# Second layer of a graph transformer: slot sums by TensorE in place of VectorE, and the norm's inverse root by Newton steps in place of logarithm and exponential

## The chip, the cores and the metric

One core of a Trainium2 chip runs the whole program. The metric is the device time of one execution in microseconds. Engines are named as the profile names them: PE (TensorE), DVE (VectorE), ACT (ScalarE), POOL (GpSimd) and SP (SyncE, which here only issues transfers).

## The reference

A graph of 6250 nodes and 100000 edges (sorted by destination), 16 node types, 32 edge types, width 128 in 8 heads of 16. Two layers of this, then a final linear layer, a residual and a norm:

```python
def gt_layer(x, ntype, etype, src, dst, Wk, Wq, Wv, Wa, Watt, Wmsg, pri, skip, g, b):
    k = typed_linear(x, ntype, Wk).reshape(n, H, HS)
    q = typed_linear(x, ntype, Wq).reshape(n, H, HS)
    v = typed_linear(x, ntype, Wv).reshape(n, H, HS)
    kT = jnp.einsum('nhd,htdo->nhto', k, Watt)
    vT = jnp.einsum('nhd,htdo->nhto', v, Wmsg)
    kw = kT[src, :, etype]
    m = vT[src, :, etype]
    a = jnp.einsum('ehd,ehd->eh', kw, q[dst]) * pri[:, etype].T / SQRT_D
    att = edge_softmax(a, dst, n)
    msg = (m * att[:, :, None]).reshape(-1, H * HS)
    hag = jax.ops.segment_sum(msg, dst, num_segments=n)
    h = jax.nn.silu(typed_linear(hag, ntype, Wa))
    alpha = jax.nn.sigmoid(skip[ntype])[:, None]
    h = h * alpha + x * (1.0 - alpha)
    mu = jnp.mean(h, axis=-1, keepdims=True)
    var = jnp.mean((h - mu) ** 2, axis=-1, keepdims=True)
    return (h - mu) * jax.lax.rsqrt(var + 1e-05) * g + b
...
h = x
for l in range(L):
    h = gt_layer(h, ...)
return layernorm(x + (h @ ff_w + ff_b))
```

## The kernel before

**Tables and blocks.** For each layer the kernel writes a table in HBM with a row of 256 floats (transformed key and value) for each pair of node and edge type. Nodes are ranked by type class and by number of edges and put into 50 blocks of 128. A block has a fixed number of slots, K, one per edge of its node with the most edges: 25, 22, 20, 19, 18, 17, 16, 16, 15 and 14 for the ten blocks of each of four type classes, then one of 41 and nine of 13 down to 8. All blocks together have 867 slots. Blocks are taken in 15 superblocks of three or four. In order of execution their slots are [25, 22, 20, 19], [18, 17, 16], [16, 15, 14], [41, 13, 12], then a class and [12, 12, 11], a class and [11, 10, 9, 8], and the last class.

**The edge loop** (`edges`, once for each layer) goes over the blocks. A slot is one indirect gather of 128 rows of the table, issued by POOL (L987). Four slots make a chunk, a tile `kv` of which 12 exist. DVE multiplies the key halves by the query (L999) and reduces them to scores (L1003). When a block's scores are there, `finished` does the softmax over slots: mask (L898), maximum (L903), difference (L905), exponential on ACT (L908), its sum `den` (L911); then, chunk by chunk, the value halves are multiplied by the weights (L922), the chunks are added (L929), and the four remaining slots are reduced to `sums` (L932). `finished` of one block is a generator that is advanced three times for each chunk of the next block.

In the second layer a block has a tile `pair` of two PSUM banks (pool `tps`, three of them, tile name `tb`). Its second bank holds the query and, behind it, the weights; its first bank holds `acc`, the four partial sums. The first chunk is multiplied into `acc`, later ones in place in `kv`. In the first layer these stand in SBUF.

**Node steps.** When a superblock's sums are ready, `nodes` divides them by `den` (`normalized`, L1030 to L1037) and does the type-dependent product (`typed_linear`, L238 and L247, with masked copies `xm`), the activation (L1085, L1092), the skip (L1099), mean and variance (`stats`, L1066, L1069), the inverse root (`rstd_of`) and the norm (L1106, L1110). In the first layer it goes on to the second layer's keys, values and queries and, in `pieces_of`, to that layer's table: PE products (L268) into `tb`, ACT copies (L275) into `st`, scatters by POOL (L1198). In the second layer it does the final product (L1175 to L1177; L1177 adds the input row by a product with the identity), a second norm and an output scatter by POOL (L1231). These steps are advanced between the steps of the edge loop: `spread` gives a generator's steps a rate, a number of steps over the slots of a coming superblock.

**Order.** POOL's instructions stand in the order in which the program issues them. The other engines' orders are made by the scheduler when the program is built; each engine then runs its list in order and waits on semaphores.

Of the kernel before, what the change touches and what calls it, by code (L numbers as in the profile page):

```python
# [9 lines left out]
F32 = mybir.dt.float32  # L10
BF16 = mybir.dt.bfloat16
I32 = mybir.dt.int32
AF = mybir.ActivationFunctionType
ALU = mybir.AluOpType
AX = mybir.AxisListType
# [3 lines left out]
P = 128  # L19
# [4 lines left out]
LN_EPS = 1e-5  # L24

SB = 4
# [5 lines left out]
CH = 4  # L32
# [64 lines left out]
def kernel(  # L97
# [21 lines left out]
    nc = tc.nc  # L119
    N, D = out.shape  # L120
# [4 lines left out]
    L, TY, _, _ = Wk.shape  # L125
    _, H, RT, HS, _ = Watt.shape
    HP = H // 2
    TG = RT // 16
    TC = TY // NC
# [29 lines left out]
    ident = keep.tile([P, P], F32, name="ident")  # L159
# [5 lines left out]
    start = keep.tile([P, NB], I32, name="start")  # L165
# [60 lines left out]
    def superblocks(n):  # L226
        k = -(-n // SB)
        for c in range(k):
            yield n * c // k, n * (c + 1) // k - n * c // k
# [150 lines left out]
    with tc.If(unsorted > 0):  # L380
# [7 lines left out]
        with tc.For_i(0, EC, 1) as j:  # L388
            pair = pp.tile([P, 2], I32, name="pair")
# [57 lines left out]
    with tc.tile_pool(name="tp", bufs=2) as tp, \  # L447
# [304 lines left out]
        sbs = list(superblocks(NT))  # L752
# [26 lines left out]
    def arm(fast):  # L779
# [4 lines left out]
        STB = 3 if fast else 2  # L784
        ep = ctx2.enter_context(tc.tile_pool(name="ep", bufs=2))
        npl = ctx2.enter_context(tc.tile_pool(name="npl", bufs=1))
        eps = npl.tile([P, 1], F32, name="eps")
        nc.vector.memset(eps, LN_EPS)

        nps = ctx2.enter_context(tc.tile_pool(name="nps", bufs=2 if fast else 5, space=PSUM))  # L790
        tps = ctx2.enter_context(tc.tile_pool(name="tps", bufs=3, space=PSUM))
# [2 lines left out]
        sbs = []  # L794
# [7 lines left out]
        else:  # L802
            sbs = [(i0, k, range(TY)) for i0, k in superblocks(NB)]
# [40 lines left out]
        def edges(l):  # L844
# [8 lines left out]
            def spread(work, gen, steps, slots):  # L853

                work.append([gen, steps / slots, 0.0])
# [24 lines left out]
            def slots(s):  # L880
                return sum(KB[b] for b in range(sbs[s][0], sbs[s][0] + sbs[s][1]))

            def query(s, i):


                if l == 0:
                    return got[s][0][:, i, :], None
                pair = tps.tile([P, 2, SB * P], F32, name="tb")
                nc.scalar.copy(pair[:, 1, :D], got[s][0][:, i, :])  # L889
                return pair[:, 1, :D], pair  # L890

            def finished(s, i, chunks, kvt, a, pair, sums, den):


                i0, k, _ = sbs[s]
                K = KB[i0 + i]
                av = a[:, :K, :]
                nc.vector.tensor_tensor(  # L898
                    av, av, neg[:, KO[i0 + i]:KO[i0 + i] + K].unsqueeze(2)
                    .to_broadcast([P, K, H]), op=ALU.add)  # L900
                yield
                m = ep.tile([P, H], F32, name="m")
                nc.vector.tensor_reduce(m, av.rearrange("p k h -> p h k"), axis=AX.X, op=ALU.max)  # L903
                yield
                nc.vector.tensor_tensor(av, av, m.unsqueeze(1).to_broadcast([P, K, H]),  # L905
                                        op=ALU.subtract)
                w = av if l == 0 else pair[:, 1, D:D + K * H].rearrange("p (k h) -> p k h", h=H)
                nc.scalar.activation(w, av, AF.Exp)  # L908
                yield
                yield  # L910
                nc.vector.tensor_reduce(den[:, i, :], w.rearrange("p k h -> p h k"),  # L911
                                        axis=AX.X, op=ALU.add)

                if l == 0:
                    acc = ep.tile([P, CH, D], F32, name="acc", bufs=1)
                else:
                    acc = pair[:, 0].rearrange("p (k c) -> p k c", k=CH)
                for j in range(len(chunks) + 1):
                    if j < len(chunks):
                        j0, j1 = chunks[j]  # L920
                        v = kvt[j][:, :j1 - j0, D:]
                        nc.vector.tensor_tensor(  # L922
                            (v if j else acc).rearrange("p k (h d) -> p k h d", h=H),
                            v.rearrange("p k (h d) -> p k h d", h=H),
                            w[:, j0:j1, :].unsqueeze(3).to_broadcast([P, j1 - j0, H, HS]),
                            op=ALU.mult)
                    if j > 1:
                        j0, j1 = chunks[j - 1]
                        nc.vector.tensor_tensor(acc[:, :j1 - j0], kvt[j - 1][:, :j1 - j0, D:],  # L929
                                                acc[:, :j1 - j0], op=ALU.add)  # L930
                    yield
                nc.vector.tensor_reduce(sums[:, i, :], acc.rearrange("p k c -> p c k"),  # L932
                                        axis=AX.X, op=ALU.add)
                if i == k - 1:
                    spread(work, nodes(l, *sbs[s], sums, den, got[s][1], lambda gen: table(s, gen)),
                           36 if l else 27 + (12 if len(sbs[s][2]) > TC else 0), pace(s + 1))

            def pace(s):
                s = min(s, len(sbs) - 1)
                return slots(s) - 0.5 * KB[sbs[s][0]]  # L940
# [3 lines left out]
            def table(s, gen):  # L944


                if gen is None:
                    if s - 2 in tables:
                        rush(pieces, tables[s - 2])
                else:  # L950
                    tables[s] = gen
                    spread(pieces, gen, 8 * sbs[s][1] + 4, (1.0 if s + 4 < len(sbs) else 0.6) * slots(min(s + 2, len(sbs) - 1)))

            before = iter(())
            q, pair = query(0, 0)
            for s, (i0, k, types) in enumerate(sbs):
# [4 lines left out]
                sums = ep.tile([P, SB, D], F32, name="sums")  # L961
                den = ep.tile([P, SB, H], F32, name="den")
                for i in range(k):
                    b = i0 + i
                    K = KB[b]
                    a = ep.tile([P, max(KB), H], F32, name="a")
                    chunks = [(j, min(j + CH, K)) for j in range(0, K, CH)]
                    kvt = []
# [12 lines left out]
                    for j0, j1 in chunks:  # L981
                        c = j1 - j0
                        kv = ep.tile([P, CH, 2 * D], F32, name="kv", bufs=12)
                        kvt.append(kv)
                        for j in range(j0, j1):
                            at = KO[b] + j
# [3 lines left out]
                            if l == 1:  # L990
                                for put in puts:
# [13 lines left out]
                                                axis=AX.X, op=ALU.add)  # L1005
# [7 lines left out]
                    if not then:  # L1013
                        step(end=True)
                    before = finished(s, i, chunks, kvt, a, pair, sums, den)
                    q, pair = then[0] if then else (None, None)
            for _ in before:
# [25 lines left out]

        def rstd_of(mv, k):

            rs = npl.tile([P, SB], F32, name="rs")
            nc.scalar.activation(rs[:, :k], mv[:, :k, 1], AF.Ln, bias=eps)
            v = npl.tile([P, SB], F32, name="v")
            nc.vector.tensor_scalar(v[:, :k], mv[:, :k, 1], LN_EPS, -0.5, op0=ALU.add, op1=ALU.mult)
            yield  # L1050
            nc.scalar.activation(rs[:, :k], rs[:, :k], AF.Exp, scale=-0.5)
            yield
            t = npl.tile([P, SB], F32, name="t")
            nc.vector.tensor_tensor(t[:, :k], rs[:, :k], rs[:, :k], op=ALU.mult)
            yield
            nc.vector.tensor_tensor(t[:, :k], t[:, :k], v[:, :k], op=ALU.mult)
            yield
            nc.vector.scalar_tensor_tensor(rs[:, :k], t[:, :k], 1.5, rs[:, :k],
                                           op0=ALU.add, op1=ALU.mult)
            yield  # L1060
            return rs

        def stats(mv, what, k):
# [8 lines left out]
        def nodes(l, i0, k, types, sums, den, ntb, table):  # L1072
# [29 lines left out]
            yield  # L1102
            yield from stats(mv, lambda i: hs[:, i, :], k)
            rs = yield from rstd_of(mv, k)
            for i in range(k):
                nc.vector.scalar_tensor_tensor(hs[:, i, :], hs[:, i, :], mv[:, i, 0:1], gt[:, l],  # L1106
# [66 lines left out]
            for i in range(k):  # L1173
# [4 lines left out]
            yield  # L1178
            yield from stats(mv, lambda i: f[:, i * P:(i + 1) * P], k)
            rs = yield from rstd_of(mv, k)  # L1180
            o = npl.tile([P, SB * P], F32, name="o", tag="kvT0", bufs=2).rearrange(
                "p (i d) -> p i d", i=SB)
# [140 lines left out]
    with tc.If(full < 1) as cmp:  # L1323
        with ExitStack() as ctx2:
            ctx2.enter_context(tc.manual_schedule(engines={mybir.EngineType.Pool}))
            arm(True)
    with cmp.Else():
        with ExitStack() as ctx2:
            arm(False)
# [46 lines left out]
```

## Time and profile before

| | |
|---|---|
| median of 3 runs | 3465.71 us (3457.21 to 3470.19) |
| the profiled execution | 3457.21 us |
| its span | 3455.4 us |
| PE busy | 1937.8 us (56%) |
| DVE busy | 2165.0 us (63%) |
| ACT busy | 978.7 us (28%) |
| POOL busy | 2002.5 us (58%) |
| mean granted TensorE clock | 0.72 of full speed |

Busy time of an engine counts its instructions, not the gaps in which it issues or waits. Three stages follow each other: table building for the first layer to about 700 us (POOL's first table gather starts at 817 us), the first layer's edge loop to 2240 us, and the second layer's to the end. In a list of instruction groups a row gives line, engine, operation, output and input tiles, count, then busy time and mean duration in ns, then the engine's idle time ahead of them and what ended it. In the timeline a row gives start, duration, engine, line, instruction, and in brackets the idle time before it.

### The profile page before, as it was taken

The numbers are of one execution on the slowest core, as the hardware profiler recorded it, in microseconds if no ns is written. First come the engines' busy times: TensorE is split into PE (matmuls) and PEld (weight loads), VectorE is DVE, ScalarE is ACT, GpSimd is POOL, SyncE is SP. The second block draws the span as 40 slices with busy tenths as digits, with TensorE's granted clock in tenths as the row PEclk, the third lists the DMA queues.
The fourth block names the chain that finished last, engine by engine and source line by source line (L and its number), as shares of the span: only waits on it lengthen the run. The fifth ranks groups of instructions, "written<-read, shape, count | busy, mean of one in ns | idle before, by whom it ended". The sixth has DMA issues, their size and how long they took to land. (4 is left out here: it accounts for less than half of the span.)

```text
span 3455.4 us, 25373 instructions
## 1 busy us (share of the span) xinstructions
PE 1937.8 (56%) x7142; PEld 874.0 (25%) x7142; DVE 2165.0 (63%) x4496; ACT 978.7 (28%) x1594; POOL 2002.5 (58%) x2032
## 2 busy tenths in 40 slices
PE   6999999894057676777778777602112222121313
PEld 3444454332022232333233223201001111011111
DVE  5787786332575677666666765346656666566765
ACT  2444433452014313442344245401111111021111
POOL 0000003644767777767767776177767777777773
PEclk9999999995577677877777877755555555555555
DMA  7676655889338656885688478734333333333331
GB/s 198 277 301 285 273 244 213 316 343 292 99 115 290 221 189 223 292 289 189 226 290 317 164 280 328 317 107 113 110 99 109 111 112 106 111 117 110 110 106 49
DMA packets 201147, 694.53 MB, mean 201 GB/s; under 512 B 61383, under 2 KB 111897, under 8 KB 175947
## 3 DMA queue, kind: packets, MB, share of 16 engines
q0 software_dynamic: 105424, 448.83, 39.1%
q1 hardware_dynamic: 79182, 236.82, 17.8%
q10 hardware_dynamic: 16384, 7.11, 0.9%
q8 instruction: 60, 0.98, 0.1%
q14 instruction: 97, 0.79, 0.1%
HBM read 268.12 MB, written 429.48 MB: 202 GB/s over the span
## 5 line engine op out<-in xcount | busy, mean ns | idle before, releaser
L987 POOL DMA_INDIRECT kv<-tab,ell x1734 | 1708.7, 985 | 618.8 <-issue 471.4
L275 ACT COPY st<-tb 128x512 f32<-128x512 f32 (+1 forms) x976 | 681.0, 764 | 602.9 <-PE tb L268 515.9
L253 PE MATMUL nb<-ident,hag 128*128 128x128 f32 x100 | 26.1, 399 | 767.1 <-DVE hag L1037 750.9
L739 PE MATMUL l<-xm,wkqv 128*128 128x512 f32 (+1 forms) x832 | 383.1, 595 | 31.7 <-DVE xm L238 31.7
L999 DVE TENSOR_TENSOR kv<-kv,tb 128x512 f32<-128x512 f32 (+3 forms) x234 | 150.5, 645 | 381.3 <-DMA kv<-tab,ell 368.4
L999 DVE TENSOR_TENSOR kv<-kv,q 128x512 f32<-128x512 f32 (+3 forms) x234 | 151.6, 650 | 352.9 <-DMA kv<-tab,ell 345.1
L268 PE MATMUL tb<-bdv,kvT 32*128 32x512 f32 x800 | 268.4, 795 | 67.0 <-ACT st L275 65.9
L1003 DVE TENSOR_REDUCE a<-kv 128x32 f32<-128x512 f32 (+3 forms) x468 | 297.3, 638 | 2.2
L247 PE MATMUL nb<-xm,wa 128*128 128x384 f32 (+1 forms) x384 | 214.3, 720 | 83.7 <-DVE xm L238 83.6
L268 PE MATMUL tb<-bdk,kvT 32*128 32x512 f32 x800 | 241.9, 781 | 23.5 <-ACT st L275 23.1
L273 DVE COPY st<-tb 128x512 f32<-128x512 f32 (+1 forms) x208 | 149.0, 717 | 117.1 <-PE tb L268 96.0
L238 DVE SCALAR_TENSOR_TENSOR xm<-ntb,hT 128x512 f32<-128x512 int32 (+1 forms) x208 | 133.3, 656 | 131.7 <-PE l L739 103.2
L238 DVE SCALAR_TENSOR_TENSOR xm<-ntb,nb 128x384 f32<-128x384 bf16 (+1 forms) x336 | 185.6, 591 | 47.5 <-PE nb L253 31.6
L253 PEld LDWEIGHTS nb<-ident,hag 128*128 128x128 f32 x100 | 15.6, 197 | 785.3 <-issue 576.6
L739 PEld LDWEIGHTS l<-xm,wkqv 128*128 128x128 f32 x832 | 148.0, 192 | 261.8 <-issue 195.9
L1198 POOL DMA_INDIRECT tab<-st,row x100 | 107.9, 1079 | 149.4 <-ACT st L275 102.9
L727 POOL DMA_DIRECT2D ntb<-in_node_type_dram x13 | 7.3, 559 | 317.2 <-DVE xm L238 317.2
L247 PE MATMUL nb<-xm,wq 128*128 128x384 f32 (+1 forms) x192 | 104.0, 707 | 138.4 <-DVE xm L238 138.4
L268 PE MATMUL tb<-bdv,yT 32*128 32x512 f32 x784 | 169.2, 663 | 2.5 <-DVE st L273 2.2
L889 ACT COPY tb<-q 128x128 f32<-128x128 f32 x50 | 13.4, 269 | 469.8 <-DVE sums L932 346.8
L247 PEld LDWEIGHTS nb<-xm,wa 128*128 128x128 f32 x384 | 95.6, 262 | 200.1 <-DVE xm L238 115.2
L1132 PE MATMUL nb<-xm,wkqv 128*128 128x384 f32 (+1 forms) x288 | 125.2, 585 | 33.2 <-DVE xm L238 22.6
(243 smaller groups left out, 3009.6 us busy)
## 6 DMA issues: line engine op xcount, KB each, us to landing
tab<-st SPq DMA_DIRECT2D x98, 2048.0 KB, 6.7
kv<-tab,ell POOLq DMA_INDIRECT x1734
hr<-xrd SPq DMA_DIRECT2D x30, 192.0 KB, 3.9
hr<-xrd SPq DMA_DIRECT2D x15, 256.0 KB, 7.3
xrd<-xr POOLq DMA_DIRECT2D x11, 256.0 KB
hr<-in_x_dram POOLq DMA_DIRECT2D x10, 256.0 KB
ntb<-in_node_type_dram POOLq DMA_DIRECT2D x10, 256.0 KB
ntb<-typed SPq DMA_DIRECT2D x20, 96.0 KB, 3.2
```

Source lines behind the costliest of these rows:

```text
L238: nc.vector.scalar_tensor_tensor(xm[:, :n], ntb[:, :n], float(t), hT[:, :n], op0=ALU.is_equal, op1=ALU.mult)
L247: nc.tensor.matmul(ps[:, :n], w[:, t, :], xm[:, :n], start=(t == types[0]), stop=(t == types[-1]))
L253: nc.tensor.transpose(tr[:, i * P:(i + 1) * P], src_of(i), ident)
L268: nc.tensor.matmul(pt[:, b], yT[s, i * P:(i + 1) * P], bd[s, tt, :], start=True, stop=True)
L273: nc.vector.tensor_copy(to, pt)
L275: nc.scalar.copy(to, pt)
L739: nc.tensor.matmul(ps[i][:, :n], wkqv[:, i, t, :], xm[:, :n], start=(t == 0), stop=(t == TY - 1))
L987: get = nc.gpsimd.indirect_dma_start(out=kv[:, j - j0, :], out_offset=None, in_=tabs[l][:], in_offset=bass.IndirectOffsetOnAxis(ap=ell[:, ...
L999: nc.vector.tensor_tensor(kk, kk, q.unsqueeze(1).to_broadcast([P, c, D]), op=ALU.mult)
L1003: nc.vector.tensor_reduce(a[:, j0:j1, :], kk.rearrange("p k (h d) -> p k h d", h=H), axis=AX.X, op=ALU.add)
L1132: nc.tensor.matmul(outs[j][:, :n], wkqv[:, j, t, :], xm[:, :n], start=(t == types[0]), stop=(t == types[-1]))
L1198: put = nc.gpsimd.indirect_dma_start(out=tabs[1].rearrange("(n t) c -> n (t c)", t=16), out_offset=bass.IndirectOffsetOnAxis(ap=row2[:, tg ...
```

## The change

In the second layer each value chunk is multiplied in place, the first one too. The sum over slots is then one product per slot of the identity and the slot's 128 values, accumulated in the first bank of `pair`, issued in the step after the chunk's multiplication; ACT copies the result to `sums`. The adds and the reduction on DVE remain for the first layer alone. In `rstd_of`, in both layers, the logarithm and the exponential on ACT with one Newton step on DVE are replaced by an integer first guess and three Newton steps on DVE. The numbers of steps given to `spread` become 34 (27 before) and 50 (36 before).

```diff
-        eps = npl.tile([P, 1], F32, name="eps")
-        nc.vector.memset(eps, LN_EPS)
...
                 if l == 0:
                     acc = ep.tile([P, CH, D], F32, name="acc", bufs=1)
-                else:
-                    acc = pair[:, 0].rearrange("p (k c) -> p k c", k=CH)
                 for j in range(len(chunks) + 1):
                     if j < len(chunks):
                         j0, j1 = chunks[j]
                         v = kvt[j][:, :j1 - j0, D:]
                         nc.vector.tensor_tensor(
-                            (v if j else acc).rearrange("p k (h d) -> p k h d", h=H),
+                            (acc if l == 0 and not j else v).rearrange("p k (h d) -> p k h d", h=H),
                             v.rearrange("p k (h d) -> p k h d", h=H),
                             w[:, j0:j1, :].unsqueeze(3).to_broadcast([P, j1 - j0, H, HS]),
                             op=ALU.mult)
-                    if j > 1:
+                    if l == 1 and j > 0:
+                        j0, j1 = chunks[j - 1]
+                        for at in range(j0, j1):
+                            nc.tensor.matmul(pair[:, 0, :D], ident, kvt[j - 1][:, at - j0, D:],
+                                             start=(at == 0), stop=(at == K - 1))
+                    if l == 0 and j > 1:
                         j0, j1 = chunks[j - 1]
                         nc.vector.tensor_tensor(acc[:, :j1 - j0], kvt[j - 1][:, :j1 - j0, D:],
                                                 acc[:, :j1 - j0], op=ALU.add)
                     yield
-                nc.vector.tensor_reduce(sums[:, i, :], acc.rearrange("p k c -> p c k"),
-                                        axis=AX.X, op=ALU.add)
+                if l == 0:
+                    nc.vector.tensor_reduce(sums[:, i, :], acc.rearrange("p k c -> p c k"),
+                                            axis=AX.X, op=ALU.add)
+                else:
+                    nc.scalar.copy(sums[:, i, :], pair[:, 0, :D])
                 if i == k - 1:
                     spread(work, nodes(l, *sbs[s], sums, den, got[s][1], lambda gen: table(s, gen)),
-                           36 if l else 27 + (12 if len(sbs[s][2]) > TC else 0), pace(s + 1))
+                           50 if l else 34 + (12 if len(sbs[s][2]) > TC else 0), pace(s + 1))
...
         def rstd_of(mv, k):
-            rs = npl.tile([P, SB], F32, name="rs")
-            nc.scalar.activation(rs[:, :k], mv[:, :k, 1], AF.Ln, bias=eps)
             v = npl.tile([P, SB], F32, name="v")
-            nc.vector.tensor_scalar(v[:, :k], mv[:, :k, 1], LN_EPS, -0.5, op0=ALU.add, op1=ALU.mult)
-            yield
-            nc.scalar.activation(rs[:, :k], rs[:, :k], AF.Exp, scale=-0.5)
-            yield
+            nc.vector.tensor_scalar(v[:, :k], mv[:, :k, 1], LN_EPS, None, op0=ALU.add)
+            yield
+            gi = npl.tile([P, SB], I32, name="gi")
+            nc.vector.tensor_single_scalar(gi[:, :k], v[:, :k].bitcast(I32), 1,
+                                           op=ALU.arith_shift_right)
+            yield
+            ri = npl.tile([P, SB], I32, name="ri")
+            nc.vector.tensor_scalar(ri[:, :k], gi[:, :k], -1.0, float(0x5F3759DF),
+                                    op0=ALU.mult, op1=ALU.add)
+            nc.vector.tensor_scalar(v[:, :k], v[:, :k], -0.5, None, op0=ALU.mult)
+            yield
+            rs = ri.bitcast(F32)
             t = npl.tile([P, SB], F32, name="t")
-            nc.vector.tensor_tensor(t[:, :k], rs[:, :k], rs[:, :k], op=ALU.mult)
-            yield
-            nc.vector.tensor_tensor(t[:, :k], t[:, :k], v[:, :k], op=ALU.mult)
-            yield
-            nc.vector.scalar_tensor_tensor(rs[:, :k], t[:, :k], 1.5, rs[:, :k],
-                                           op0=ALU.add, op1=ALU.mult)
-            yield
+            for _ in range(3):
+                nc.vector.tensor_tensor(t[:, :k], rs[:, :k], rs[:, :k], op=ALU.mult)
+                yield
+                nc.vector.tensor_tensor(t[:, :k], t[:, :k], v[:, :k], op=ALU.mult)
+                yield
+                nc.vector.scalar_tensor_tensor(rs[:, :k], t[:, :k], 1.5, rs[:, :k],
+                                               op0=ALU.add, op1=ALU.mult)
+                yield
             return rs
```

## The prediction

> **What bounds the kernel now.** I read the busy time by stage first, because a share over the whole span mixes three stages: table building (to about 700 us), first layer (to 2240 us) and second layer (to the end).
>
> ```profile
> core 0: us, PE busy (x) PEld busy (x) DVE busy (x) ACT busy (x) POOL busy (x), PEclk, DMA share, GB/s
> 700.00:2240.00 1540.00, 1049.46 (x3222) 430.98 (x3222) 936.47 (x1914) 558.27 (x781) 1028.70 (x1002) 0.75 0.70 248
> 2240.00:3455.00 1215.00, 251.15 (x642) 147.37 (x642) 751.68 (x1812) 148.55 (x293) 873.52 (x917) 0.54 0.36 105
> ```
>
> In the second layer no engine looks full: POOL 72%, DVE 62%, PE 21%. The groups of instructions for that stretch explain POOL:
>
> ```profile
> L987 POOL DMA_INDIRECT kv<-tab,ell x867 | 822.7, 949 | 291.3 <-issue 243.2 <-DVE tb L922 8.9 <-DVE tb L929 5.0
> ```
>
> There are 867 gathers of 0.949 us, and before nearly each of them a gap of 0.30 us in which POOL waits for nothing ("issue"). So a gather costs 1.25 us: 867 x 1.25 = 1084 us, and 50 output scatters at 1.3 us add 65. That is 1149 of 1215 us; about 45 us are the tail behind the last gather, and real waits of POOL come to about 20. **POOL's issue is the bound of the second layer**; DVE, PE and ACT matter only where they release a gather buffer late, and in the tail. The timeline shows where they do (start, duration, instruction, idle time before it):
>
> ```profile
> 2541.83 0.69 DVE L922 TENSOR_TENSOR tb<-kv,tb 128x512 f32<-128x512 f32 x1
> 2542.48 0.80 PE L1175 MATMUL nb<-ffw,h 128*128 128x128 f32 x2 [0.57 <-ACT h L1171]
> 2542.55 1.28 DVE L922 TENSOR_TENSOR kv<-kv,tb 128x512 f32<-128x512 f32 x2
> 2542.79 0.94 POOL L987 DMA_INDIRECT kv<-tab,ell  x1 [7.65 <-DVE tb L922]
> ...
> 2631.99 0.67 DVE L922 TENSOR_TENSOR tb<-kv,tb 128x512 f32<-128x512 f32 x1
> 2632.93 0.94 POOL L987 DMA_INDIRECT kv<-tab,ell  x1 [1.60 <-DVE v L1049]
> 2633.23 1.27 DVE L922 TENSOR_TENSOR kv<-kv,tb 128x512 f32<-128x512 f32 x2
> 2637.47 0.94 POOL L987 DMA_INDIRECT kv<-tab,ell  x1 [2.35 <-DVE t L1056]
> ```
>
> With 12 chunk buffers, a chunk's first gather needs the chunk 12 places before it to be read for the last time. The 41-slot block (11 chunks) and the 25-slot blocks (7 chunks) run out: six waits of 7.65, 2.27, 1.60, 2.35, 1.72 and 2.35 us, of which 0.30 each is issue. I paired every chunk with its predecessor: beside these six and the chunks right behind them the margin is 2.5 us at the last 25-slot block, 8.3 at the first, and 10 us or more elsewhere.
>
> In the first layer POOL is also ahead of the others (1029 of 1540 busy, plus 0.30 us for each issue), but it has real waits, most of them in scatters of the second table:
>
> ```profile
> POOL tab L1198 <- ACT st L275: 102.9, 25, 14.7
> L1047 ACT ACT_TABLE_LOAD x6 | 7.7, 1283 | 0.1
> ```
>
> (POOL's waits from 700 to 2300 us: total, number, longest; then table loads in one window of the layer, 1300 to 1800 us: 6 of 1283 ns, as many again at L1051.)
>
> **The change, part by part.** The sum is made on the profiled execution, 3457.2 us (span 3455.4); the median of the runs is 3465.7, so 8.5 us are added at the end.
>
> *Taken from DVE in layer 2.* 185 adds (L929, 0.632 us) are 117 us and 50 reductions (L932, 0.678) are 34. Newton adds 9 instructions per norm of about 0.157 us (rows of L1054, L1056, L1058), 30 norms: 42 us. DVE falls by 109 us of 752. On the path this is worth 0: POOL's 1.25 us per gather hides it. Were POOL's gathers free, DVE would be next and the 109 us would count.
>
> *Given to PE.* 867 products of the identity with a 128x128 fp32 slot. The same shape and operands stand at L1177, among the final products:
>
> ```profile
> 3434.61 0.79 PE L1175 MATMUL nb<-ffw,h 128*128 128x128 f32 x2 [0.57 <-ACT h L1171]
> 3435.33 0.79 PE L1176 MATMUL nb<-ffb,one_row 1*128 1x128 f32 x2
> 3436.06 0.80 PE L1177 MATMUL nb<-hr,ident 128*128 128x128 f32 x2
> 3436.64 0.64 PE L1175 MATMUL nb<-ffw,h 128*128 128x128 f32 x2
> ```
>
> Nine such products take 5.99 us from 3434.61 to 3440.60 (the last one's end): 0.665 us each, 2.66 for a chunk of four. So PE gains 577 us and stands at 828 of 1215, below POOL. The other end of the price: at the first layer's higher granted clock (0.75 against 0.54) 5.5 products of 512 columns took 4.88 us (0.89 each), where second-layer ones take 1.68; half, hence 0.33 and 1.33 for a chunk. I take 0.665, the row of this shape in this stage.
>
> [...]
>
> *The new wait.* The program's waits tie both engines together through the tile that holds weights and sums: the products of chunk j wait for DVE's multiplication of chunk j+1, and the multiplication of chunk j+2 waits for those products. What queues behind a waiting multiplication is all of DVE: the next block's scores and the norms. With 0.1 us for each hand-over a link costs 2.86 us; there are 235 chunks less two per block, 135 links. If nothing lay between, DVE would wait 386 us, and 752 - 109 + 386 = 1029 is still under 1215. So DVE does not become the bound; only lateness of releases counts.
>
> *Releases.* 41-slot block: the first buffer was free at the end of its multiplication (2542.5). Now it needs the second multiplication (2543.2), then PE, whose queue has nine final products in front, from 2542.48 on (9 x 0.665, to 2548.5), then 2.66: 2551.1. The wait grows by 8.6; the later 2.27 goes (the chain then needs 3.4 us a chunk where gathers need 5.0); six more Newton steps in front cost 1. Together +8; without the queue +2, at 0.33 us about 0. 25-slot blocks: 2633.9 + 0.1 + 2.66 = 2636.6, and with the 0.30 us of issue the gather starts 5.2 us late instead of 1.3, but the second wait (2.05) goes: +1.9 each for two of them, about +1 for the one with 2.5 us of margin, 0 for the first. Sum +13. Bounds: 0, if PE runs at 0.33; +53, if at all four 25-slot blocks PE's node products (5.2 us for the type products, 6.0 for the final ones) stand in front, 4 x 11.2 + 8.
>
> *Tail.* The last block has 14 slots, chunks of 4, 4, 4, 2. Before, from its first multiplication to its sum: 3414.09 to 3419.24, 5.15 us. After: 1.25 + 2.76 + 0.65 + 2.76 + 0.4 + 2.76 + 1.43, and 0.4 for ACT's copy: 12.4, so +7.3; of the previous block's adds and reduction, 2.6 us that stood in front, I credit half: +6. At 0.33: 0. The norm itself: 13 dependent steps at 0.19 us (L1054 to L1058 start 0.19 to 0.20 apart) are 2.5 us, the chain over ACT took 2.5 (3441.54 to 3444.01): 0.
>
> *Layer 1.* ACT loses 30 table loads (38.5 us) and 30 short activations of 0.30 and 0.20 us (7.5): 46 of 558 busy us, hidden by POOL except where a scatter waits for ACT's copies. In the drain before layer 2 the norm ended at 2188.93, 6.7 us after its mean and variance (copies and two loads in ACT's queue); 2.5 now: -4.2. Of the earlier waits only that of 4.46 us at 1434 has a load and a logarithm inside it: -1.6. The node steps become 34 and 50 in place of 27 and 36 for the same slots, so some scatters move past one chunk in POOL's queue, 5 us either way. I take -6; bounds -46 (all of ACT's saving on the path) and +10 (two scatters caught early).
>
> [...]
>
> **Sum:** -6 + 13 + 6 + 0 = +13: 3470 for an execution like the profiled one, **3479** beside the median. 0.5% (17 us) is about what a measurement of this kernel can tell from no change.
>
> **Rivals.** *Slower:* PE's node products stand in front of the slot sums at every tight buffer; it decides where lateness passes the margins (0, 2.5, 8.3 us). For it: PE's order is fixed when the program is built. Against: a 25-slot block ends before the final products are due. -6 + 53 + 6 = +53: 3519. *Faster:* ACT's copies were what held the scatters, and all 46 us that ACT saves come off the 102.9 us of waits. For: 25 waits name ACT. Against: most follow type products on PE, with no load near. -46 + 13 + 6 = -27: 3439. *PE at the higher clock:* -6 + 0 + 0: 3460.
>
> **Numbers.** Chances: my sum 0.45, slower rival 0.33, faster rival 0.15, higher clock 0.07. Of my sum 0.06 lies beyond +17 and of the higher clock 0.01 beyond -17, so slower 0.39, same 0.45, faster 0.16. Range 3440 to 3525, from the faster rival to just past the slower one; about half of each of the two lies outside.
>
> **What would show it.** Second layer: gathers still 0.95 us with 0.30 before; POOL's waits now name PE's slot sums, 25 to 40 us in total in place of 20; PE about 830 busy; L929 and L932 gone; one or two table loads left. First layer: waits for ACT's copies near 100 us. It is wrong if a gather's cadence changes, if POOL waits for PE at ordinary blocks, or if the layer boundary moves by more than 15 us.

## The result

The changed kernel takes 3479.52 us (median of 20 runs, 3470.95 to 3489.29), the kernel before 3466.7 us beside it (20 runs, 3457.21 to 3476.15). The ratio is 1.0036, 95% interval [1.0026, 1.0047]: 12.8 us more, inside the 0.5% that was forecast as no change. The profiled execution took 3484.13 us (span 3482.3).

The time was met; the sum behind it was not. These are the stages of the profiled executions, read off POOL's timeline (the one before was the fastest of its 20, and 4.6 us of the difference of 26.9 between the two are the start's):

| us | before | after | foreseen |
|---|---|---|---|
| start to POOL's first table gather | 817.2 | 821.8 | 0 |
| first layer: to the second layer's first gather | 1423.0 | 1444.5 (+21.5) | -6 |
| second layer: first to last gather | 1161.6 | 1163.2 (+1.6) | +13 |
| tail: last gather to the end of the last output scatter | 46.5 | 45.5 (-1.0) | +6 |

The engines' busy times by stage, and the groups and waits of the second layer of the changed kernel, stand against the rows of before in the prediction:

```profile
core 0: us, PE busy (x) PEld busy (x) DVE busy (x) ACT busy (x) POOL busy (x), PEclk, DMA share, GB/s
700.00:2266.00 1566.00, 1050.46 (x3218) 440.47 (x3214) 949.87 (x2047) 512.07 (x718) 1045.68 (x1004) 0.74 0.69 244
2266.00:3475.00 1209.00, 609.87 (x2376) 486.05 (x2376) 648.85 (x1848) 69.52 (x223) 873.50 (x917) 0.60 0.37 105
```

```profile
L991 POOL DMA_INDIRECT kv<-tab,ell x867 | 822.7, 949 | 288.2 <-issue 217.3 <-PE tb L926 37.7 <-DVE kv L1003 4.6
...
L926 PE MATMUL tb<-kv,ident 128*128 128x128 f32 x1734 | 394.5, 404 | 470.1 <-DVE kv L918 376.4 <-issue 89.0 <-ACT hb L1100 2.5
```

```profile
POOL tab L1209 <- ACT st L275: 114.3, 25, 25.7
POOL out_dram L1242 <- DVE o L1195: 42.6, 4, 24.1
POOL kv L991 <- PE tb L926: 37.7, 81, 13.0
```

(The last three are POOL's waits: total, number, longest; the first from 700 to 2300 us, the other two in the second layer.) The edit did what it says: PE has 1734 more records (two for each of 867 products), ACT fell to 70 us, DVE from 752 to 649. The gathers are the same 867 of 949 ns. Of the 81 waits for PE's sums most are the 0.30 us of issue that were there before; the real one is that of 13.0 us. The second layer is still bound by POOL's issue, and so all this work moved at a cost of 0.6 us. What was lost was lost in the first layer, which this edit touches through the Newton steps, one step number (34 for 27) and the order that the scheduler makes of them.

### Where the second layer's numbers came from

The one long wait is the 41-slot block's (timeline of the changed kernel: start, duration, instruction, idle time before it):

```profile
2566.78 0.80 PE L1186 MATMUL nb<-ffw,h 128*128 128x128 f32 x2 [0.57 <-ACT h L1182]
...
2568.39 1.27 DVE L918 TENSOR_TENSOR kv<-kv,tb 128x512 f32<-128x512 f32 x2
...
2572.57 1.91 PE L926 MATMUL tb<-kv,ident 128*128 128x128 f32 x8
2574.52 0.69 DVE L918 TENSOR_TENSOR kv<-kv,tb 128x512 f32<-128x512 f32 x1 [0.80 <-PE tb L926]
2574.76 0.94 POOL L991 DMA_INDIRECT kv<-tab,ell  x1 [12.95 <-PE tb L926]
```

As foreseen, the nine final products stand in front of the slot sums and POOL waits for both: 12.95 + 0.63 us in place of 7.65 + 2.27, +3.7. What the second layer got in addition are two output scatters that wait, 0.80 and 4.40 us; this is the longer one:

```profile
2924.82 1.01 POOL L1242 DMA_INDIRECT out_dram<-o,node  x1 [4.40 <-DVE o L1195]
```

At the 25-slot blocks the four waits of before are gone. The first of them, DVE and ACT alone, before and after:

```profile
2621.94 0.34 ACT L908 ACTIVATE tb<-a 128x200 f32<-128x200 f32 x1
...
2623.60 0.69 DVE L999 TENSOR_TENSOR kv<-kv,tb 128x512 f32<-128x512 f32 x1 [1.25 <-DMA kv<-tab,ell]
2628.19 0.69 DVE L999 TENSOR_TENSOR kv<-kv,tb 128x512 f32<-128x512 f32 x1 [3.90 <-DMA kv<-tab,ell]
2628.79 0.55 DVE L1092 SCALAR_TENSOR_TENSOR th<-th,nb 128x384 f32<-128x384 f32 x1
2629.26 0.36 DVE L911 TENSOR_REDUCE den<-tb 128x8 f32<-128x200 f32 x1
```

```profile
2652.69 0.34 ACT L906 ACTIVATE tb<-a 128x200 f32<-128x200 f32 x1
2653.18 0.54 DVE L1103 SCALAR_TENSOR_TENSOR th<-th,nb 128x384 f32<-128x384 f32 x1
2653.64 0.36 DVE L909 TENSOR_REDUCE den<-tb 128x8 f32<-128x200 f32 x1
2653.91 0.68 DVE L918 TENSOR_TENSOR kv<-kv,tb 128x512 f32<-128x512 f32 x1
...
2658.52 0.69 DVE L1003 TENSOR_TENSOR kv<-kv,tb 128x512 f32<-128x512 f32 x1 [1.04 <-DMA kv<-tab,ell]
```

Before, the block's first weighting (2631.99) came 10.1 us after its exponential, because DVE's list put it behind two score multiplications that wait 1.25 and 3.90 us for gathers, and behind some node steps. After, it comes 1.2 us behind. That is a new order in DVE's list, made when the program is built; it pays for the longer chain through PE.

The last block, DVE's multiplication of its last chunk by the query, before and after, then the rest of the changed kernel's chain:

```profile
3409.96 0.41 DVE L999 TENSOR_TENSOR kv<-kv,tb 128x256 f32<-128x256 f32 x1
```

```profile
3432.34 0.42 DVE L1003 TENSOR_TENSOR kv<-kv,tb 128x256 f32<-128x256 f32 x1 [3.36 <-DMA kv<-tab,ell]
3435.28 0.68 DVE L918 TENSOR_TENSOR kv<-kv,tb 128x512 f32<-128x512 f32 x1
...
3437.40 6.82 PE L926 MATMUL tb<-kv,ident 128*128 128x128 f32 x38 [2.20 <-DVE kv L918]
...
3446.42 0.27 ACT L937 COPY sums<-tb 128x128 f32<-128x128 f32 x1 [2.75 <-PE tb L926]
```

From the first weighting to the sums 11.4 us, in place of 5.15 (foreseen 12.4). But the first weighting comes 5.8 us after the start of the last gather (3429.44), in place of 12.3 (3401.76 to 3414.09). Before, DVE came to the last score multiplication 8.2 us after that gather's start and had not waited; after, it sat idle for the gather and was there 2.9 us after its start. The adds and the reduction of the block ahead are 2.6 us of what no longer stands in front; its weightings and a superblock's norm and output, which stood there too, now come earlier or later in DVE's list.

### The profile page after: what moved, and what is told of

Read it like the earlier page. It is cut to its first block, busy times and chain, and to the rows that moved or that the text cites. A ratio compares the mean times of both kernels' runs of the same rounds, so it can differ in the third digit from the quotient of the medians.

```text
span 3482.3 us, 29131 instructions
## 1 busy us (share of the span) xinstructions
PE 2298.3 (66%) x8876; PEld 1222.0 (35%) x8876; DVE 2076.2 (60%) x4666; ACT 854.9 (25%) x1464; POOL 2016.5 (58%) x2032
## 5 line engine op out<-in xcount | busy, mean ns | idle before, releaser
L991 POOL DMA_INDIRECT kv<-tab,ell x1734 | 1726.4, 996 | 619.7 <-issue 447.5
L926 PE MATMUL tb<-kv,ident 128*128 128x128 f32 x1734 | 394.5, 404 | 470.1 <-DVE kv L918 376.4
L926 PEld LDWEIGHTS tb<-kv,ident 128*128 128x128 f32 x1734 | 350.8, 301 | 516.7 <-DVE kv L918 347.7
L1003 DVE TENSOR_TENSOR kv<-kv,tb 128x512 f32<-128x512 f32 (+3 forms) x234 | 151.1, 646 | 487.3 <-DMA kv<-tab,ell 473.5
L268 PE MATMUL tb<-bdv,kvT 32*128 32x512 f32 x800 | 272.9, 820 | 67.4 <-ACT st L275 66.5
L268 PE MATMUL tb<-bdk,kvT 32*128 32x512 f32 x800 | 243.4, 781 | 12.5 <-ACT st L275 12.1
L247 PE MATMUL nb<-xm,wa 128*128 128x384 f32 (+1 forms) x384 | 201.9, 687 | 61.5 <-DVE xm L238 61.5
L1209 POOL DMA_INDIRECT tab<-st,row x100 | 104.6, 1046 | 154.6 <-ACT st L275 114.3
L247 PE MATMUL nb<-xm,wq 128*128 128x384 f32 (+1 forms) x192 | 105.6, 714 | 131.9 <-DVE xm L238 122.2
L918 DVE TENSOR_TENSOR kv<-kv,tb 128x512 f32<-128x512 f32 (+3 forms) x234 | 147.4, 638 | 37.2 <-PE tb L926 37.2
L268 PE MATMUL tb<-bdv,yT 32*128 32x512 f32 x784 | 166.7, 654 | 2.9 <-ACT st L275 1.8
L247 PEld LDWEIGHTS nb<-xm,wa 128*128 128x128 f32 x384 | 92.6, 252 | 167.2 <-DVE xm L238 88.0
L1162 PE MATMUL nb<-xm,wkqv 128*128 128x384 f32 (+1 forms) x288 | 134.0, 626 | 16.6 <-DVE xm L238 16.4
```

The lines of the kernel that those rows point to most:

```text
L247: nc.tensor.matmul(ps[:, :n], w[:, t, :], xm[:, :n], start=(t == types[0]), stop=(t == types[-1]))
L268: nc.tensor.matmul(pt[:, b], yT[s, i * P:(i + 1) * P], bd[s, tt, :], start=True, stop=True)
L918: nc.vector.tensor_tensor((acc if l == 0 and not j else v).rearrange("p k (h d) -> p k h d", h=H), v.rearrange("p k (h d) -> p k h d", h=H ...
L926: nc.tensor.matmul(pair[:, 0, :D], ident, kvt[j - 1][:, at - j0, D:], start=(at == 0), stop=(at == K - 1))
L991: get = nc.gpsimd.indirect_dma_start(out=kv[:, j - j0, :], out_offset=None, in_=tabs[l][:], in_offset=bass.IndirectOffsetOnAxis(ap=ell[:, ...
L1003: nc.vector.tensor_tensor(kk, kk, q.unsqueeze(1).to_broadcast([P, c, D]), op=ALU.mult)
```

## The experiments

On record stood theory 1, the prediction's own terms, and theory 2, read from the profile after: the slot sums cost the second layer nothing, the loss is the first layer's, by the pace of its steps (2a) or by the Newton instructions and the new order they bring (2b). Times are ratios to the kernel before on the same chip; stages are from one profiled execution each. The first four ran on a chip on which the kernel before took 3898 us, so the questions were put again on two others, at 3467 and 3468 us.

**The kernel before, as it is** (before_same).

> The kernel before itself, unchanged: its ratio shows what this comparison tells from no change (1.000 within 0.001 by every theory), and its profile gives the stage times on the same chip as the kernels run beside it. The first four runs were on a chip on which the kernel before took 3898 us; there its stages were not profiled.

Ratio 0.9997 [0.9982, 1.0012]. First layer 1422.7, second 1207.9 (before: 1423.0, 1208.1): the two layers repeat within 0.3 us. How the second divides does not: its gathers took 1162.3 and its tail 45.6 (before: 1161.6 and 46.5), so the -1.0 of the table's tail is no difference, and half of its +1.6 may be none. Nor does the start repeat: 826.9 in place of 817.2, and from 817 to 829 over the profiled executions of all kernels. So ten us of difference between two spans can be the start's, and stages are compared from the first gather on.

**Slot sums on PE alone** (pe_sums, pe_sums2). The changed kernel's `edges` with the old `rstd_of` and the old step numbers:

```diff
+                    if l == 1 and j > 0:
+                        j0, j1 = chunks[j - 1]
+                        for at in range(j0, j1):
+                            nc.tensor.matmul(pair[:, 0, :D], ident, kvt[j - 1][:, at - j0, D:],
+                                             start=(at == 0), stop=(at == K - 1))
-                    if j > 1:
+                    if l == 0 and j > 1:
...
+                    nc.scalar.copy(sums[:, i, :], pair[:, 0, :D])
```

> The kernel before with the slot sums of the second layer on TensorE alone; the norm and the step numbers 36 and 27 as before. Theory 1 (the terms of the prediction: releases +13, tail +6, first layer -6): second layer longer by 19 us from its first gather to the end, first layer unchanged, ratio to before 1.0055. Theory 2 (the profile of the changed kernel: the slot sums cost the second layer nothing, what is lost is lost in the first layer): second layer within 3 us of before's 1208, first layer unchanged, ratio 0.998 to 1.001.

> The kernel before with the slot sums on TensorE alone, as in the run pe_sums, for a chip on which the kernel before takes near 3466 us. Theory 1: second layer longer by 19 us, ratio 1.0055. Theory 2: second layer within 3 us, ratio 0.998 to 1.001. On a chip like that of the first runs (3898 us, where GpSimd waited 280 us and more in the second layer): second layer longer by 25 to 35 us, ratio near 1.010 as there.

pe_sums2: 1.0009 [0.9996, 1.0022]; first layer 1426.9 (+4, though its code is that of before), second 1209.8 (gathers 1163.3, tail 46.5). Theory 1's +19 in the second layer falls. The 41-slot wait is 12.99 + 0.70 here too, and of the four 25-slot waits one of 3.67 is left: DVE's order changed with the slot sums alone. pe_sums, on the other chip: 1.0103 [1.0078, 1.0127]; second layer 1456, where the two kernels with DVE's sums run beside it took 1425. There POOL waited 314 us beyond issue in the second layer (pe_sums2: 70), and 282 and 283 in those two kernels, newton and before_pace26: on that chip the chain through PE cost some 31 us and was not free. Why that chip is slower stays open.

**Newton steps alone** (newton, newton2). The changed kernel's `rstd_of` and step numbers 34 and 50, sums on DVE.

> The kernel before with the Newton steps and the step numbers 50 and 34; slot sums on VectorE as before. Theory 1: first layer -6 us, second layer +0, ratio 0.998. Theory 2: the first layer, from its first gather to the second layer's first gather, is longer by 13 to 21 us, waits of GpSimd for the table copies of ScalarE near 114 us with one near 25 us; ratio 1.004 to 1.006.

> The kernel before with Newton steps and the step numbers 34 and 50, as in the run newton, for a chip near 3466 us. Theory 1: first layer -6 us, ratio 0.998. Theory 2: first layer longer by 10 to 21 us, second layer within 3 us, ratio 1.003 to 1.006.

newton2: 1.0002 [0.9986, 1.0019], which neither theory had. First layer 1436.6, +14 as theory 2 said, with a wait of 25.8 us like the changed kernel's; but second layer 1198.9, -9.0, as all four 25-slot waits went. newton, on the other chip: 1.0073 [1.0046, 1.0099].

The two parts explain the second layer. Both remove the same four waits of the 25-slot blocks (6.7 us beyond issue): the Newton kernel all of them, the slot sums alone half (3.4 are left), both together all of them once. Together they also have what neither has alone, the two output scatters that wait 0.80 and 4.40 us. So 3.7 - 6.8 + 4.6 = +1.5 (issue taken off), and 1.6 was measured for the gathers.

**The pace in the first layer** (before_pace26, before_pace26b): the kernel before with one number changed, so that its node steps finish at 0.85 of a superblock's slots, as in the changed kernel (29 steps at 34; before: 22 at 27, 0.81).

```diff
-                           36 if l else 27 + (12 if len(sbs[s][2]) > TC else 0), pace(s + 1))
+                           36 if l else 26 + (12 if len(sbs[s][2]) > TC else 0), pace(s + 1))
```

> The kernel before with 26 in place of 27 steps in the first layer, so that the node steps finish at 0.85 of a superblock's slots, as in the changed kernel, and nothing else. Theory 2a: first layer longer by 10 to 20 us, ratio 1.003 to 1.006. Theories 1 and 2b: ratio 1.000 within 0.002.

> The kernel before with 26 in place of 27 steps in the first layer and nothing else, as in the run before_pace26, for a chip near 3466 us. Theory 2a (pacing alone makes the loss): first layer longer by 10 to 20 us, ratio 1.003 to 1.006, near that of newton2. Theory 2b (the Newton instructions make it): ratio 1.000 within 0.002.

before_pace26b: 1.0039 [1.0026, 1.0053], first layer 1446.4 (+23.5), second 1206.7; on the other chip 1.0046 [1.0025, 1.0067]. Without a Newton step or a slot sum on PE, one number costs what the whole change costs, a little more than 2a said. The third superblock shows how, in the timeline of the kernel before (before_same), then of before_pace26b:

```profile
1023.75 2.84 ACT L275 COPY st<-tb 128x1024 f32<-128x1024 f32 x3
1024.81 2.15 PE L268 MATMUL tb<-bdv,kvT 32*128 32x512 f32 x4 [7.01 <-ACT st L275]
1026.89 13.07 PE L247 MATMUL nb<-xm,wq 128*128 128x384 f32 x32
1027.00 1.01 ACT L275 COPY st<-tb 128x1024 f32<-128x1024 f32 x1 [0.41 <-PE tb L268]
1028.29 1.99 POOL L1198 DMA_INDIRECT tab<-st,row  x1 [8.07 <-ACT st L275]
...
1045.49 1.01 POOL L1198 DMA_INDIRECT tab<-st,row  x1 [10.18 <-ACT st L275]
```

```profile
1023.84 1.93 ACT L275 COPY st<-tb 128x1024 f32<-128x1024 f32 x2 [1.42 <-PE tb L268]
1024.58 2.07 PE L268 MATMUL tb<-bdv,kvT 32*128 32x512 f32 x2
1026.58 12.51 PE L247 MATMUL nb<-xm,wq 128*128 128x384 f32 x32
1039.02 1.13 PE L268 MATMUL tb<-bdv,kvT 32*128 32x512 f32 x6
...
1042.39 1.02 POOL L1198 DMA_INDIRECT tab<-st,row  x1 [25.36 <-ACT st L275]
```

The first scatter of a table piece needs its four value products (L268, two records each). Before, all four stand in front of the query products (L247, 13 us). At the new pace one does and three stand behind: POOL waits 25.4 us where two waits made 18.3. The order of PE's records there in the traces, counted in products (bdv: value products, wq: query products):

```
before, pe_sums, after_pace36, newton_pace36, before_l2pace32:   bdv x4 | wq x16 |
changed kernel, newton:                                          bdv x2 | wq x16 | bdv x2
before_pace26:                                                   bdv x1 | wq x16 | bdv x3
```

The third superblock, where this lies, takes 90.2 us with the first order (91.1 and 89.7 in after_pace36b and before_l2pace32; 95.1 in newton_pace36, though), and 97.4, 98.1 and 96.5 with the other two. It is a third of the loss. Superblock by superblock (from its first gather to the next one's), against before:

| us | third | eighth | twelfth | fourteenth | the other eleven together |
|---|---|---|---|---|---|
| before_same | +0.1 | +0.5 | +0.5 | +1.4 | -2.8 |
| changed kernel | +7.2 | -5.5 | +7.4 | +11.9 | +0.5 |
| before_pace26b | +6.3 | -6.1 | +8.5 | +7.1 | +7.7 |
| after_pace36b (below) | +0.9 | -2.4 | +0.4 | +2.3 | -0.9 |

The twelfth has the same pattern. Before, its four value products stand in front of the query products and no scatter waits; in the changed kernel they are split:

```profile
1820.41 3.75 PE L247 MATMUL nb<-xm,wq 128*128 128x512 f32 x4 [4.50 <-DVE xm L238]
1824.09 1.23 PE L268 MATMUL tb<-bdv,kvT 32*128 32x512 f32 x2
1825.25 1.98 PE L247 MATMUL nb<-xm,wq 128*128 128x512 f32 x4
1827.16 1.12 PE L268 MATMUL tb<-bdv,kvT 32*128 32x512 f32 x2
1829.61 1.01 POOL L1209 DMA_INDIRECT tab<-st,row  x1 [6.62 <-ACT st L275]
```

In the eighth it is the kernel before that has them split, with a wait of 7.6 us that the new pace takes away. In the fourteenth this order does not settle it: two value products stand ahead in the kernel before and in before_pace26b, which loses 7.1 us there all the same, and one in the changed kernel. The rest was not read, and no run changed the order at one of these places alone.

**The changed kernel at the old pace** (after_pace36, after_pace36b).

```diff
-                           50 if l else 34 + (12 if len(sbs[s][2]) > TC else 0), pace(s + 1))
+                           50 if l else 36 + (11 if len(sbs[s][2]) > TC else 0), pace(s + 1))
```

> The changed kernel with 36 (and 11 more in the mixed superblocks) in place of 34 (and 12) steps in the first layer, so that the node steps finish at the same share of a superblock's slots as in the kernel before (0.81 and 0.89, where 34 gives 0.85 and 0.91). Theory 1: 1.003, as the changed kernel. Theory 2a (the lower pace of the steps starts the table pieces later): the first layer comes back to within 5 us of before's 1423 us, ratio 0.998 to 1.000. Theory 2b (the Newton instructions themselves, or the scheduler's new order, make the loss): ratio stays at 1.003 to 1.005.

> The changed kernel with 36 (and 11 more in the mixed superblocks) in place of 34 (and 12) steps in the first layer, as in the run after_pace36, for a chip near 3466 us. Theory 2a (the first layer's loss comes from the pace: its node steps finished at 0.85 of a superblock's slots and finish here at 0.81, as before): first layer back from 1444.5 to 1423 to 1428 us, second layer as the changed kernel's 1209, ratio 0.998 to 1.001. Theory 2b (the Newton instructions and the scheduler's new order make it): first layer 1437 to 1446, ratio 1.002 to 1.005.

after_pace36b: first layer 1423.3, second 1211.0; 1.0016 [1.0002, 1.0029]. The stage came back whole, as 2a said; the Newton instructions alone do not make the loss. The ratio fell by less and lies between the two forecasts: 0.2%, 7 us, where the profiled stages fell by 19. From the first gather on, the profiled executions of the changed kernel and of before_pace26b lie 22 us above the kernel before, their medians 13 and 14; for the other kernels on this kind of chip stages and medians agree within 5. So the place of the loss is read from the stages, and its size from the medians: 7 us between these two kernels, 14 for before_pace26b. after_pace36 on the other chip: 1.0157 [1.0123, 1.0192], first layer 1666, as long as before_pace26's 1665 there. The changed kernel itself did not run on that chip, so what the old pace is worth there is not known; it did not bring the first layer back to the 1631 of pe_sums.

**Newton at other paces** (newton_pace36: 36 and 11 in the first layer; newton_pace40_57: 40 and 13, and 57 in the second).

> Newton steps, slot sums on VectorE, steps 36 (and 11) in the first layer, 50 in the second. Theory 2a: first layer 1423 to 1428 (newton2 with 34: 1436.6), second layer 1199 as newton2, ratio 0.9965 to 0.9985, faster than both kernels. Theory 2b: first layer 1436 and more, ratio 1.000.

> Newton steps, slot sums on VectorE, steps 40 (and 13) in the first layer, 57 in the second: the node steps finish at 0.73 of a superblock's slots in the first layer (before 0.81) and at 0.67 in the second (as before). First layer: if finishing earlier is better throughout, under 1423; if only the place chosen before is good, over 1430. Second layer: 1199 if Newton makes the gain, 1208 if the pace does. Ratio 0.995 to 1.005 by these.

newton_pace36: 0.9996 [0.9982, 1.0011], first layer 1431.7, second 1200.8; it lies between 2a and 2b and is no gain. Its first layer has the same instructions and step numbers as that of after_pace36b, and took 8.4 us more in its profiled execution: only the second layer's code differs. So something counts beside the pace and the Newton instructions. PE's order at the third and the twelfth superblock is the same in both, and what it is was not found. newton_pace40_57: 1.0003 [0.9987, 1.002], first layer 1424.7, second 1201.0. The first layer lies between its two cases too: an earlier finish is neither better throughout nor bad. The second layer keeps its gain at the old pace of 0.67.

**The second layer's pace alone** (before_l2pace32): `32 if l else 27` in the kernel before.

> The kernel before with 32 in place of 36 steps in the second layer alone, so that its node steps finish at 0.75 of a superblock's slots, as with Newton and 50 (0.76; before 0.67). If the gain of 9 us in newton2's second layer came from this pace: second layer 1199, no waits at the 25-slot blocks, ratio 0.9975. If it came from the Newton steps (no logarithm and exponential for VectorE to wait for): second layer 1207 to 1209, ratio 1.000.

0.9977 [0.9963, 0.9991]; first layer 1424.5, second 1201.8, waits at the 25-slot blocks 1.45 + 0.45 in place of 1.55 + 2.35. So the pace alone gains 6 of the 9 us, and, by newton_pace40_57, the Newton steps alone 7. They do it by different orders of DVE's list. With Newton the first weighting comes 3.0 us after the exponential; here it still comes 9.9 us after, the first wait stays, and the second goes because the first add now stands in front of the step that waits for ACT's inverse root:

```profile
2641.13 0.68 DVE L929 TENSOR_TENSOR tb<-kv,tb 128x512 f32<-128x512 f32 x1
2642.45 0.16 DVE L1054 TENSOR_TENSOR t<-rs 128x3 f32<-128x3 f32 x1 [0.64 <-ACT rs L1051]
```

This kernel, one number away from the kernel before, is the fastest of all that ran: 9 us below it, and by the two ratios 0.6% below the changed one.

## Why the prediction was right, and where it was not

- **Bound of the second layer:** right. The cadence of 0.95 + 0.30 us stayed, 103 us of DVE and 79 of ACT went and 359 of PE came without an effect of their own. (The trace has 184 adds and 234 chunks, one fewer of each than the prediction's sums; that moves no term by 1 us, but for the 386 us of links, which are 383.)
- **Price of a product:** the step that failed took 0.665 us from nine products in which three kinds take turns. A chunk of four took 2.07 us in place of 2.66, and one link of the chain (weighting, hand-over, products) 2.86 us, where the tail's sum had 3.4. PE stands at 610, not 828. The products of the row started 0.57 to 0.73 us apart, those of a chunk 0.43.
- **Releases, +13:** +1.6, of which 0.7 is what the unchanged kernel showed too. The 41-slot block's mechanism was right (foreseen +8, measured +3.7: the final products started 1.6 us ahead of the weighting and not 0.7 after). The 25-slot blocks were wrong in sign (foreseen +4.8, measured -6.8). The step that failed let the weighting stand where it stood before; DVE's list had been rebuilt. The two output scatters (+4.6) were not in the sum.
- **Tail, +6:** -1.0. The chain grew by 6.3, close to the 7.3 foreseen; the step that failed is the credit for the work in front, 1.3 us, where the weighting came 6.5 us earlier.
- **The norm, 0:** right: 2.4 us in the last norm from mean and variance to the root's use (3468.32 to 3470.73), 2.5 before.
- **First layer, -6:** +21.5 in the profiled execution, some 12 by the medians. The step that failed is "some scatters move past one chunk in POOL's queue, 5 us either way". It looked at POOL's queue only; the pace also moved the value products behind 13 us of query products in PE's. The boundary between the layers moved by more than 15 us, which the prediction had named as a sign that it is wrong. Its term of -4.2 in the drain was right: the last norm ahead of the second layer took 2.8 us after mean and variance in place of 6.7, and from the last gather of the first layer to the first of the second it is 79.7 to 80.2 us in after_pace36b, newton_pace36 and newton_pace40_57, 83.7 to 86.9 in the kernels without Newton; at the step number 34 it was lost again (83.7 and 84.7). More of ACT's saving (512 us busy in place of 558) showed nowhere: POOL's waits for the copies rose from 102.9 to 114.3 us, and where a long one was read, it was a wait for PE behind the copies, which the prediction had said against its faster rival.
- **The rivals.** Lateness, the slower one's ground, did cost where the slack is gone: on the chip at 3898 us the slot sums cost the second layer 31 us, though its waits were not paired with PE's node products. The faster one fell with the first layer. The clock did rise at times, in the last block for one (0.60 as the second layer's mean, 0.54 before). The second layer's +0.6 is what the rival with the higher clock foresaw, but not for its reason: most chunks took 2.07 us and not 1.33.
- **The sum, +13:** 12.8 by the medians, 22 by the profiled stages. Errors of -11 and -7 us in the second layer stood against one of 18 to 28 in the first. Why the profiled stages show more than the medians stays open. The median lies in the range; that 3479 was met to a microsecond is chance. The 17 us taken for what a measurement can tell was too wide: the interval is 0.1% to either side, and 12.8 us is clear of it.

## What to carry to other kernels

Where steps are dealt out at a pace, a change in their number is a change of its own: keep the share at which they finish, and test the numbers alone. Before pricing a wait, read the built order of every engine around the tight places, not of the queue that is known to wait. Parts that remove the same wait do not add up, and a kernel whose time was foreseen can still have been misread: only the stages tell.

## What the runs showed of the hardware

The TensorE clock rose in the middle of a run of slot products. Windows of pe_sums2 around its last block:

```profile
core 0: us, PE busy (x) PEld busy (x) DVE busy (x) ACT busy (x) POOL busy (x), PEclk, DMA share, GB/s
3427.00:3430.00 3.00, 2.07 (x8) 1.78 (x8) 2.00 (x9) 0.89 (x2) 0.00 (x0) 0.50 0.01 3
3430.00:3436.00 6.00, 5.19 (x23) 4.90 (x24) 2.61 (x7) 0.27 (x1) 3.00 (x3) 0.52 0.10 33
3436.00:3440.00 4.00, 2.63 (x20) 2.25 (x20) 0.94 (x2) 0.27 (x1) 0.00 (x0) 1.00 0.00 0
```

After 5.1 us of products without a gap (from 3430.03) and a pause of 0.8 us the granted clock stood at 1.0 in place of 0.5. In the changed kernel it rose within one run of 38 records: 0.213 us from one to the next from 3437.4 to 3442.0, then 0.112. Chunks of eight records with pauses between mostly took 2.07 us. But the length of a run is not all of it. The row just ahead of that run, slot products with nine final products among them, kept 0.5 for 8.4 us; its records start 0.21 to 0.38 us apart:

```profile
3426.80:3435.20 8.40, 8.39 (x29) 6.75 (x29) 3.74 (x11) 0.74 (x2) 2.95 (x3) 0.50 0.19 57
3437.40:3442.00 4.60, 4.60 (x21) 4.60 (x22) 2.72 (x13) 0.00 (x0) 0.00 (x0) 0.50 0.01 2
3442.00:3444.00 2.00, 2.00 (x19) 2.00 (x17) 1.81 (x8) 0.27 (x1) 0.32 (x1) 0.93 0.00 0
```

So at these two places the clock rose after 4.6 and 5.1 us of products, and in the row of 8.4 us it did not; what sets the moment, no run shows.

A second-layer gather takes 949 ns in both kernels, in the changed one beside 270 more small Newton instructions and 234 fewer adds and reductions on DVE.
